# A graph layer's columns and maxima spread over partitions through DRAM instead of TensorE, with one buffer of reciprocals and nine of exponentials

## The chip, the core and the metric

The kernel runs on one core of a Trainium2 chip. A core has a matrix engine (TensorE, PE in the profile), a vector engine (VectorE, DVE), a scalar engine (ScalarE, ACT), GpSimd (POOL) and SyncE (SP), which here only issues DMAs. Each engine works through its own queue of instructions; semaphores between the queues keep the data in order. SBUF is the on-chip memory of 128 partitions, PSUM the memory that matmuls write into, DRAM the large memory outside. A DMA moves data between DRAM and SBUF or inside SBUF. The metric is the time of the kernel on the device in microseconds (us); lower is better.

## What is computed

The input x holds 32 independent items of 512 nodes with 512 features; adj is a 512 x 512 adjacency that all items share. Two layers follow each other, each with a residual and a layer norm:

```python
def layer0(X, A, W, a):                       # W: 512 x 256, a: 2 x 256 x 1
    h = einsum('bnf,fo->bno', X, W)
    e = einsum('bno,od->bnd', h, a[0]) + swapaxes(einsum('bno,od->bnd', h, a[1]), 1, 2)
    e = leaky_relu(e, 0.2) - 1e9 * (1 - A)
    alpha = softmax(e, axis=-1)
    return concatenate([einsum('bij,bjo->bio', alpha, h), h], axis=-1)

def layer1(h, adj, Wq, bq, Wk, bk, Wv, bv, Wo, bo):      # 8 heads of 64
    q, k, v = heads(h @ Wq.T + bq), heads(h @ Wk.T + bk), heads(h @ Wv.T + bv)
    s = where(adj == 0, -inf, einsum('bhqd,bhkd->bhqk', q, k) / 8)
    return merge(einsum('bhqk,bhkd->bhqd', softmax(s), v)) @ Wo.T + bo

x = layernorm(x + layer0(x, adj, W, a))
x = layernorm(x + layer1(x, adj, Wq, bq, Wk, bk, Wv, bv, Wo, bo))
```

In layer 0 the score of a pair of nodes is only a sum of two numbers, one for each node: a column "self" and a column "neigh" of 512 numbers. The change is about how such a column, which lies with one number in each partition, becomes a row that every partition holds.

## The kernel before

All arithmetic is in float32. An item b is handled whole: 512 nodes are four tiles of 128 partitions (NB = 4). The main loop runs over b, and inside it over four pairs of heads (hp = 0 to 3, "pairs" below). Into the four pairs of item b are woven layer 0 of item b + 1, the projection and column work of item b + 2, and the output projection (finish) of item b - 1, so that TensorE always has work.

The queues of TensorE, SyncE and VectorE keep the order in which the program text issues their instructions. The orders of ScalarE and GpSimd are set by the framework's scheduler, from its own estimate of when operands are ready. Tiles come from pools: `bufs` is the number of buffers behind a tag, and an instruction that writes a reused buffer waits until the earlier readers are done.

What each pair does on TensorE, in this order: scores of the tiles 0 and 1 (`ps`, head_scores), a first insert, scores of the tiles 2 and 3, then head_values of the pair before (`pav`), then a second insert. The inserts that matter here:

- pair 0: first insert l0_scores(b + 1) and project_v; second insert l0_rows(b + 1), project_v, and on other engines l0_add_h(b + 1) and l0_weights(b + 1).
- pair 1: l0_values(b + 1) (`po`), then project_two(b, 1) for the second half of the heads.
- pair 2: finish(b - 1) (`pf`).
- pair 3: store(b - 1), four l0_project(b + 2) (`ph`), then project_two(b + 1, 0) for the first heads of the next item.

For the scores VectorE takes, for each tile and head, a masked maximum out of PSUM into a tile p (tag "p"), ScalarE takes the exponential in place with its sum, and after all eight of a pair VectorE transposes them in blocks (head_blocks). Then VectorE takes the reciprocals of the sums (tot), SyncE writes them to DRAM (d_tot), and two GpSimd DMAs read them back into all partitions (inv), while SyncE issues 16 DMAs that move the transposed blocks (pt<-t). head_values of that pair, a pair later, multiplies by inv (VectorE, ot).

Layer 0 of an item:

- l0_project: `ph` = x W with two more columns for self and neigh; ScalarE copies it to h (L339 in the profile).
- l0_scores: row_of transposes a column, broadcast to 128 columns, against the identity: four matmuls of 128 x 128 leave the row of 512 numbers in every partition of a PSUM tile. `pn` is the neigh row; four masked maxima on VectorE write into throwaway tiles junk (tag "p"), and from them comes `most`, the maximum of each node. `pself` is the self row; ScalarE's Prelu adds neigh and takes the leaky ReLU into et (L366), and GpSimd adds the mask (L370).
- l0_rows: row_of turns `most` into the row `pl`.
- l0_weights: VectorE subtracts `pl` from et (L383), ScalarE takes the exponential (L384).
- l0_values: `po` = et times h, normalised and added to x by VectorE.

The tile et shares its one buffer with xt of the item after it, which l0_project reads in pair 3.

project_two computes two head pairs of q and k with seven partial products instead of eight. Its ScalarE copies p1, p5, p7 and u2 (L481) use the tag "p"; GpSimd adds p5 to p7 (L509); VectorE writes qk in four results of two operations each (L493), in the order result(0, 0), result(1, 1), result(0, 1), result(1, 0):

```python
        p7 = copy(b4, "p7")
        nc.gpsimd.tensor_tensor(p7, p7, p5, ALU.add)
        ...
        result(0, 0, b2, p1)
        product(b1, s_(1), t_(1), start=False)
        u2 = copy(b1, "u2")
        yield
        result(1, 1, b1, p7)
        product(b3, s_(2), b_(1, 1), start=False)
        yield
        result(0, 1, b3, u2)
```

The scores of the next item's pair 0 read qk of out[0], which result(0, 0) and result(0, 1) write.

Of the kernel before, what the change touches and what calls it, by code (L numbers as in the profile page):

```python
# [9 lines left out]
F32 = mybir.dt.float32  # L10
BF16 = mybir.dt.bfloat16
AF = mybir.ActivationFunctionType
ALU = mybir.AluOpType

P = 128
# [11 lines left out]
def kernel(  # L27
# [50 lines left out]
    D = F // H  # L78
    NB = N // P
    FC = F // P  # L80
    OC = F1 // P
    NP = H // 2
    SCALE = 1.0 / math.sqrt(D)
# [37 lines left out]
    st = {}  # L121
# [119 lines left out]
    def psum(name):  # L241
        return ps_m.tile([P, N], F32, name=name, tag="m")
# [98 lines left out]
    def l0_add_h(b):  # L341

        h_sb, z = st["h", b], st["x1", b]
        for i in range(NB):
            nc.gpsimd.tensor_tensor(
                z[:, i, F1:], z[:, i, F1:], h_sb[:, i, 2 : F1 + 2], ALU.add
            )

    def l0_scores(b):


        h_sb = st["h", b]
        pn = psum(f"pn_{b}")
        row_of(lambda i: h_sb[:, i, 1:2], pn)
        least = small.tile([P, NB], F32, name=f"least0_{b}", tag="least0", bufs=2)
        for i in range(NB):
            junk = prob.tile([P, N], F32, name=f"junk_{b}_{i}", tag="p", bufs=10)
            minus_max(junk, pn, mask0[:, i, :], least[:, i : i + 1])
        most = small.tile([P, NB], F32, name=f"most0_{b}", tag="most0", bufs=2)
        nc.vector.tensor_tensor(most, h_sb[:, :, 0], least, ALU.subtract)  # L360
        nc.vector.scalar_tensor_tensor(most, most, ALPHA, most, ALU.mult, ALU.max)
        pself = psum(f"pself_{b}")
        row_of(lambda i: h_sb[:, i, 0:1], pself)
        et = prob.tile([P, NB, N], F32, name=f"et_{b}", tag="et", bufs=1)
        for j in range(NB):
            nc.scalar.activation(  # L366
                et[:, j, :], pself, AF.Prelu, bias=h_sb[:, j, 1:2], alpha=ALPHA
            )
            engine = nc.vector if b == 0 and j >= 2 else nc.gpsimd
            engine.tensor_tensor(et[:, j, :], et[:, j, :], mask0t[:, j, :], ALU.add)  # L370
        st["l0", b] = et, most

    def l0_rows(b):
        _, most = st["l0", b]
        pl = psum(f"pl_{b}")
        row_of(lambda i: most[:, i : i + 1], pl)
        st["pl", b] = pl

    def l0_weights(b):
        et, _ = st["l0", b]  # L380
        pl = st.pop(("pl", b))
        for j in range(NB):
            nc.vector.tensor_tensor(et[:, j, :], et[:, j, :], pl, ALU.subtract)  # L383
            nc.scalar.activation(et[:, j, :], et[:, j, :], AF.Exp)  # L384

    def l0_values(b, i):
# [61 lines left out]
    def project_two(b, s):  # L448


        x1t, tx = st["x1t", b], st["tx", b]
        half = N // 2

        def product(ps, weights, moving, start=True):
            for k in range(2):
                for c in range(FC // 2):
                    nc.tensor.matmul(  # L457
                        ps[:, k * half : (k + 1) * half],
                        weights(k, c),
                        moving(c),  # L460
                        start=start and k == 0 and c == 0,
                        stop=c == FC // 2 - 1,
                        skip_group_check=True,
                    )

        def a_(i, f):
            cols = slice((2 * s + i) * P, (2 * s + i + 1) * P)
            return lambda k, c: (wq_sb, wk_sb)[k][:, 2 * f + c, cols]

        def s_(i):  # L470
            return lambda k, c: (wqx_sb, wkx_sb)[k][:, i, c, s, :]

        def b_(f, j):
            return lambda c: x1t[:, 2 * j : 2 * j + 2, 2 * f + c, :]

        def t_(i):
            return lambda c: tx[:, i, :, c, :]

        def copy(ps, name):
            t = prob.tile([P, N], F32, name=f"{name}_{b}_{s}", tag="p", bufs=10)  # L480
            nc.scalar.copy(t, ps)  # L481
            return t

        out = []
        for i in range(2):
            t = act.tile([P, 2, N], F32, name=f"qk_{b}_{2 * s + i}", tag="qk", bufs=2)
            st["qk", b, 2 * s + i] = t
            out.append(t)

        def result(i, j, ps, other):  # L490
            for k, bias in enumerate((bqs_sb, bk_sb)):
                cols = slice(k * half, (k + 1) * half)
                nc.vector.scalar_tensor_tensor(  # L493
                    out[i][:, k, j * half : (j + 1) * half],
                    ps[:, cols],
                    bias[:, 2 * s + i : 2 * s + i + 1],
                    other[:, cols],
                    ALU.add,
                    ALU.add,
                )  # L500

        b1, b3, b4 = (psum(f"pw{i}_{b}_{s}") for i in (1, 3, 4))
        product(b1, a_(0, 0), b_(0, 0))
        p1 = copy(b1, "p1")
        product(b3, s_(0), t_(0))
        p5 = copy(b3, "p5")
        product(b4, a_(1, 0), t_(2))
        p7 = copy(b4, "p7")
        nc.gpsimd.tensor_tensor(p7, p7, p5, ALU.add)  # L509
        b2 = psum(f"pw2_{b}_{s}")  # L510
        product(b2, a_(0, 1), b_(1, 0))
# [9 lines that stand above are left out]
        product(b4, a_(1, 1), t_(3), start=False)  # L521
        yield
        result(1, 0, b4, u2)
# [9 lines left out]
    def head_scores(b, hp, i):  # L533
        qk = st["qk", b, hp]
        if i == 0:
            st["t", b, hp] = prob.tile(
                [P, 4, 2, FC, NB, G], F32, name=f"t_{b}_{hp}", tag="t", bufs=1
            )
            st["tot", b, hp] = small.tile(
                [P, 2, NB], F32, name=f"tot_{b}_{hp}", tag="total", bufs=3  # L540
            )
        t, total = st["t", b, hp], st["tot", b, hp]
        pss = []
        for j in range(2):
            rows = slice(j * D, (j + 1) * D)
            ps = ps_s.tile([P, N], F32, name=f"ps_{b}_{hp}_{i}_{j}", tag="s")
            nc.tensor.matmul(  # L547
                ps, qk[rows, 0, i * P : (i + 1) * P], qk[rows, 1, :], start=True, stop=True
            )
            pss.append(ps)  # L550
        for j in range(2):
            name = f"{b}_{hp}_{i}_{j}"
            p = prob.tile([P, N], F32, name=f"p_{name}", tag="p", bufs=10)
            least = small.tile([P, 1], F32, name=f"least_{name}", tag="least", bufs=6)
            minus_max(p, pss[j], mask1[:, i, :], least)
            nc.scalar.activation(  # L556
                p, p, AF.Exp, bias=least, scale=-1.0, accum_out=total[:, j, i : i + 1]
            )
            st.setdefault(("p", b, hp), []).append((j, i, p))

    def head_blocks(b, hp):
        t, total = st.pop(("t", b, hp)), st.pop(("tot", b, hp))
        for j, i, p in st.pop(("p", b, hp)):
            transpose_blocks(t[:, :, j], i, p)
        nc.vector.reciprocal(total, total)
        d = dram.tile([2, P, NB], F32, name=f"d_tot_{b}_{hp}", tag="dtot")
        nc.sync.dma_start(d.rearrange("j p i -> p j i"), total)
        inv = act.tile([P, P, NB], F32, name=f"inv_{b}_{hp}", tag="inv", bufs=2)
        for j in range(2):
            nc.gpsimd.dma_start(inv[j * D : (j + 1) * D], d[j].partition_broadcast(D))  # L570
        st["inv", b, hp] = inv
        pt = prob.tile([P, 4, 2, FC, NB, G], F32, name=f"pt_{b}_{hp}", tag="pt", bufs=1)
        move_pair(pt, t)
        st["pt", b, hp] = pt
# [66 lines left out]
    masks0()  # L641
    l0_scores(0)
    l0_add_h(0)
    l0_rows(0)
    l0_weights(0)
    nc.vector.tensor_scalar(bqs_sb, bq_sb, SCALE, None, ALU.mult)
    sums = weight_sums()
# [13 lines left out]
    x1_first()  # L661
    l0_project(1, 2)
    l0_project(1, 3)
    x1_sums(0, nc.vector)
    project_v(0, 0)
    project_v(0, 1)
# [2 lines left out]
    for b in range(B):  # L669
        more = b < B - 1  # L670
        for hp in range(NP):
# [22 lines left out]
            elif hp == 2:  # L694
                if b > 0 and more:
                    finish(b - 1, 0)
                if b > 0 and more:
                    add_bias(b + 1)
            else:
                if b > 0:  # L700
                    if not more:
                        finish(b - 1, 3)
                    store(b - 1)
                if b + 2 < B:
                    for i in range(NB):
                        l0_project(b + 2, i)
                if b == 0:
                    project_v(1, 0)
            head_scores(b, hp, 2)
# [4 lines left out]
            if before is not None:  # L714
                head_values(*before)
            if hp == 0:
                if more:
                    l0_rows(b + 1)
                else:
                    project_v(b, 1)  # L720
                project_v(b, 2)
                project_v(b, 3)
# [99 lines left out]
```

## Time and profile before

| | us |
|---|---|
| median of 3 runs | 3209.63 |
| lowest and highest | 3207.91 and 3209.9 |
| the profiled execution | 3209.49 |
| span of its trace | 3207.7 |

Some groups of instructions of the trace that the change touches:

| engine, instruction | count | busy us | mean ns |
|---|---|---|---|
| TensorE L326, matmuls for pn | 128 | 20.8 | 285 |
| TensorE L326, matmuls for pself | 128 | 19.2 | 273 |
| TensorE L326, matmuls for pl | 128 | 21.7 | 294 |
| VectorE L287, junk from pn | 128 | 80.6 | 686 |
| VectorE L383, et minus pl | 128 | 79.2 | 680 |
| ScalarE L366, Prelu into et | 128 | 76.4 | 672 |
| GpSimd L370, mask added to et | 126 | 141.6 | 1156 |
| GpSimd L509, p5 added to p7 | 64 | 83.7 | 1308 |
| GpSimd L570, issue of inv | 256 | 134.4 | 528 |

The matmuls of a group overlap each other in the record, so the mean of one times the count is not the time that the group takes; that is read from the starts in a timeline. A timeline line gives the start, the length, the engine, the line of the program, the tiles and a count, and in brackets how long the engine had been idle before and what ended that. SPq is SyncE's queue of DMA issues; a DMA's landing comes later than its issue.

### The profile page before, as it was taken

Reading aid. Unit: us, or ns where it says so; the run is one execution under the profiler, and the core shown is the slowest. Engines: PE = TensorE matmul, PEld = TensorE weight load, DVE = VectorE, ACT = ScalarE, POOL = GpSimd, SP = SyncE. Lnnn points to the kernel's source line nnn. Section 1 sums busy time; section 2 is a strip of 40 time slices with the busy share of each in tenths; the row PEclk is TensorE's granted clock in tenths of the full one; section 3 lists DMA queues with packets and bytes.
Section 4 is the critical chain, followed back from the end, with each engine's and each line's share of the span. In section 5 each row is a group of like instructions: output and inputs, shape, how many; then the busy total and the mean of one; then the engine's idle time right before and its main releaser. Section 6 shows DMA issues by size and latency. Waiting matters only on the chain.

```text
span 3207.7 us, 41188 instructions
## 1 busy us (share of the span) xinstructions
PE 3163.1 (99%) x12216; PEld 1806.1 (56%) x12216; DVE 2451.1 (76%) x5665; ACT 1332.1 (42%) x3026; POOL 759.1 (24%) x869
## 2 busy tenths in 40 slices
PE   7999999999999999999999999999999999999997
PEld 5555555556556555555565565555555655655543
DVE  5788777877777877778777778877787777788775
ACT  3444443434444444434344444444343444444432
POOL 1322222221222222222222222222222122222210
PEclk9999999999999999999999999999999999999999
DMA  5565555555556555555555555555555555555554
GB/s 148 129 157 127 139 141 150 129 144 143 142 129 152 148 127 137 143 150 128 140 146 141 129 150 149 127 139 141 150 129 145 142 141 129 152 146 128 125 137 115
DMA packets 226094, 446.12 MB, mean 139 GB/s; under 512 B 81680, under 2 KB 84240, under 8 KB 225872
## 3 DMA queue, kind: packets, MB, share of 16 engines
q1 hardware_dynamic: 213408, 409.65, 50.5%
q0 software_dynamic: 12464, 33.84, 4.0%
q8 instruction: 99, 1.62, 0.2%
q14 instruction: 123, 1.01, 0.1%
HBM read 108.27 MB, written 34.08 MB: 44 GB/s over the span
## 4 chain that ended last, share of the span: by engine, by line
PE 95%; DVE 1%; SPq 1%; DMA 0%; issue 0%; ACT 0%; DVEq 0%; ACTq 0%
PE pw L457 25%; PE ps L547 15%; PE pav L582 14%; PE pv L239 14%; PE pf L603 13%; PE ph L239 7%; PE po L391 7%; SPq L319 1%; PE pl L326 1%; PE pn L326 1%; DVE t L302 0%; PE pself L326 0%; DMA pt<-t 0%; DVE p L287 0%; DVE x1t_b L302 0%
## 5 line engine op out<-in xcount | busy, mean ns | idle before, releaser
L556 ACT ACTIVATE p<-p,least 128x512 f32<-128x512 f32 x1024 | 725.9, 710 | 485.1 <-DVE least L287 416.4
L287 DVE CUSTOM_DVE_ANT_0 p<-ps,mask 128x512 f32<-128x512 f32 x1024 | 643.0, 684 | 314.0 <-PE ps L547 314.0
L302 DVE STREAM_TRANSPOSE t<-p 128x512 f32<-128x512 f32 x1024 | 621.8, 674 | 0.0
L547 PE MATMUL ps<-qk 64*128 64x512 f32 x2048 | 511.6, 615 | 2.4 <-DVE least L287 2.4
L582 PE MATMUL pav<-pt,v 128*64 128x512 f32 x2048 | 467.7, 598 | 5.3 <-DMA pt<-t 2.7
L603 PE MATMUL pf<-wo_sb,ot 128*128 128x512 f32 x1024 | 459.6, 602 | 5.6 <-DVE ot L590 5.6
L239 PE MATMUL pv<-wv_sb,x1t 128*128 128x512 f32 x1024 | 451.3, 593 | 0.0
L570 POOL DMA_DIRECT2D inv<-d_tot x256 | 134.4, 528 | 1296.2 <-DMA d_tot<-tot 712.2
L603 PEld LDWEIGHTS pf<-wo_sb,ot 128*128 128x128 f32 x1024 | 190.0, 191 | 272.4 <-issue 264.4
L547 PEld LDWEIGHTS ps<-qk 64*128 64x128 f32 x2048 | 177.8, 186 | 265.3 <-issue 207.5
L582 PEld LDWEIGHTS pav<-pt,v 128*64 128x64 f32 x2048 | 136.5, 136 | 321.1 <-issue 250.2
L239 PEld LDWEIGHTS pv<-wv_sb,x1t 128*128 128x128 f32 x1024 | 190.1, 191 | 216.0 <-issue 215.9
L239 PE MATMUL ph<-w_sb,xt 128*128 128x258 f32 x1024 | 236.9, 389 | 5.0 <-ACT x1t L422 4.7
L391 PE MATMUL po<-h,et 128*128 128x257 f32 x1024 | 232.6, 385 | 1.6 <-issue 1.6
L239 PEld LDWEIGHTS ph<-w_sb,xt 128*128 128x128 f32 x1024 | 194.8, 193 | 57.0 <-DVE mv L253 22.0
L258 ACT ACTIVATE rstd<-mv,eps 128x4 f32<-128x4 f32 (+1 forms) x70 | 20.8, 297 | 489.3 <-DVE mv L253 487.2
L391 PEld LDWEIGHTS po<-h,et 128*128 128x128 f32 x1024 | 193.4, 191 | 51.8 <-issue 25.4
L370 POOL TENSOR_TENSOR et<-et,mask0t 128x512 f32<-128x512 f32 x126 | 141.6, 1156 | 304.0 <-ACT et L366 304.0
L446 POOL TENSOR_TENSOR x<-x,bo_sb 128x512 f32<-128x512 f32 x128 | 158.4, 1269 | 190.4 <-DVE x1t_b L302 170.6
L493 DVE SCALAR_TENSOR_TENSOR qk<-pw,bqs_sb,p 128x256 f32<-128x256 f32 x128 | 61.6, 481 | 184.2 <-PE pw L457 116.7
L556 ACT ACTIVATION_READ_ACCUMULATOR p<-p,least 128x1 f32 x1024 | 191.2, 187 | 0.0
L252 DVE BATCH_NORM_STATS2 stats<-x 128x6 f32<-128x512 f32 x256 | 177.5, 693 | 13.9
(99 smaller groups left out, 3762.2 us busy)
## 6 DMA issues: line engine op xcount, KB each, us to landing
pt<-t SPq DMA_DIRECT2D x2048, 128.0 KB, 3.4
x<-in_x_dram SPq DMA_DIRECT2D x32, 1024.0 KB, 5.8
inv<-d_tot POOLq DMA_DIRECT2D x256, 128.0 KB, 3.8
xt<-in_xt_dram SPq DMA_DIRECT2D x31, 1024.0 KB, 5.4
x1t<-x1t_b SPq DMA_DIRECT2D x496, 64.0 KB, 2.0
out_dram<-x SPq DMA_DIRECT2D x31, 1024.0 KB, 4.3
d_tot<-tot SPq DMA_DIRECT2D x128, 4.0 KB, 2.1
xt<-in_xt_dram SPq DMA_DIRECT2D x4, 256.0 KB, 7.4
```

The lines of the kernel that those rows point to most:

```text
L239: nc.tensor.matmul(ps, lhs(c), rhs(c), start=(c == 0), stop=(c == FC - 1))
L252: nc.vector.bn_stats(stats, z[:, i, :])
L287: nc.vector.tensor_tensor_reduce(out=out, in0=scores, in1=mask, scale=-1.0, scalar=MIN_INIT, op0=ALU.add, op1=ALU.min, accum_out=least,)
L302: nc.vector.transpose(t[:, :, :, i, :].rearrange("p r c q -> p c r q"), src.rearrange("p (c r k) -> p c r k", r=4, k=G),)
L370: engine.tensor_tensor(et[:, j, :], et[:, j, :], mask0t[:, j, :], ALU.add)
L391: nc.tensor.matmul(po, et[:, j, i * P : (i + 1) * P], h_sb[:, j, 2:], start=(j == 0), stop=(j == NB - 1),)
L446: nc.gpsimd.tensor_tensor(z[:, i, :], z[:, i, :], bo_sb, ALU.add)
L457: nc.tensor.matmul(ps[:, k * half : (k + 1) * half], weights(k, c), moving(c), start=start and k == 0 and c == 0, stop=c == FC // 2 - 1, s ...
L547: nc.tensor.matmul(ps, qk[rows, 0, i * P : (i + 1) * P], qk[rows, 1, :], start=True, stop=True)
L556: nc.scalar.activation(p, p, AF.Exp, bias=least, scale=-1.0, accum_out=total[:, j, i : i + 1])
L582: nc.tensor.matmul(po[j * D : (j + 1) * D, :], st["v", b, c][:, head * D : (head + 1) * D], pt[:, :, j, c, :, :].rearrange("p g i q -> p g ...
L603: nc.tensor.matmul(ps, st["ot", b, c][:, i * P : (i + 1) * P], wo_sb[:, c, :], start=(c == 0), stop=(c == FC - 1),)
```

## The change

For all items but the first, the two columns and the maxima go to DRAM and come back as rows that every partition holds. SyncE writes the columns with one DMA each, one number at a time (l0_columns, behind l0_project in pair 3), and one GpSimd DMA reads both back into rows (128 x 2 x 512). The maxima go the same way from l0_scores into row. The reads of pn, pself and pl become reads of these SBUF tiles; l0_rows is gone. Item 0 keeps row_of. The exponentials have nine buffers instead of ten, inv one instead of two.

```diff
+    PB = 9
...
+    def l0_columns(b):
+
+        h_sb = st["h", b]
+        d = dram.tile([2, N], F32, name=f"d_att_{b}", tag="datt")
+        with nc.allow_non_contiguous_dma(reason="1024 numbers"):
+            for k in range(2):
+                nc.sync.dma_start(d[k].rearrange("(i p) -> p i", p=P), h_sb[:, :, k])
+        rows = prob.tile([P, 2, N], F32, name=f"rows_{b}", tag="rows", bufs=1)
+        nc.gpsimd.dma_start(rows, d.partition_broadcast(P))
+        st["rows", b] = rows
+
     def l0_scores(b):
         h_sb = st["h", b]
-        pn = psum(f"pn_{b}")
-        row_of(lambda i: h_sb[:, i, 1:2], pn)
+        if b == 0:
+            pself, pn = psum("pself"), psum("pn")
+            row_of(lambda i: h_sb[:, i, 1:2], pn)
+            row_of(lambda i: h_sb[:, i, 0:1], pself)
+        else:
+            rows = st.pop(("rows", b))
+            pself, pn = rows[:, 0], rows[:, 1]
         least = small.tile([P, NB], F32, name=f"least0_{b}", tag="least0", bufs=2)
         for i in range(NB):
-            junk = prob.tile([P, N], F32, name=f"junk_{b}_{i}", tag="p", bufs=10)
+            junk = prob.tile([P, N], F32, name=f"junk_{b}_{i}", tag="p", bufs=PB)
             minus_max(junk, pn, mask0[:, i, :], least[:, i : i + 1])
...
-        pself = psum(f"pself_{b}")
-        row_of(lambda i: h_sb[:, i, 0:1], pself)
         et = prob.tile([P, NB, N], F32, name=f"et_{b}", tag="et", bufs=1)
...
-        st["l0", b] = et, most
-
-    def l0_rows(b):
-        _, most = st["l0", b]
-        pl = psum(f"pl_{b}")
-        row_of(lambda i: most[:, i : i + 1], pl)
-        st["pl", b] = pl
+        if b == 0:
+            row = psum("pl")
+            row_of(lambda i: most[:, i : i + 1], row)
+        else:
+            d = dram.tile([N], F32, name=f"d_most_{b}", tag="dmost")
+            with nc.allow_non_contiguous_dma(reason="512 numbers"):
+                nc.sync.dma_start(d.rearrange("(i p) -> p i", p=P), most)
+            row = prob.tile([P, N], F32, name=f"row_{b}", tag="row", bufs=1)
+            nc.gpsimd.dma_start(row, d.partition_broadcast(P))
+        st["l0", b] = et, row
 
     def l0_weights(b):
-        et, _ = st["l0", b]
-        pl = st.pop(("pl", b))
+        et, row = st["l0", b]
         for j in range(NB):
-            nc.vector.tensor_tensor(et[:, j, :], et[:, j, :], pl, ALU.subtract)
+            nc.vector.tensor_tensor(et[:, j, :], et[:, j, :], row, ALU.subtract)
             nc.scalar.activation(et[:, j, :], et[:, j, :], AF.Exp)
...
-        inv = act.tile([P, P, NB], F32, name=f"inv_{b}_{hp}", tag="inv", bufs=2)
+        inv = act.tile([P, P, NB], F32, name=f"inv_{b}_{hp}", tag="inv")
...
     l0_project(1, 2)
     l0_project(1, 3)
+    l0_columns(1)
...
                     for i in range(NB):
                         l0_project(b + 2, i)
+                    l0_columns(b + 2)
...
             if hp == 0:
-                if more:
-                    l0_rows(b + 1)
-                else:
+                if not more:
                     project_v(b, 1)
```

The tiles of head_scores and project_two take `bufs=PB` in the same way.

More of the change, by code (lines that the diff above doesn't have):

```diff
@@ L479, in copy @@
         def copy(ps, name):
-            t = prob.tile([P, N], F32, name=f"{name}_{b}_{s}", tag="p", bufs=10)
+            t = prob.tile([P, N], F32, name=f"{name}_{b}_{s}", tag="p", bufs=PB)
             nc.scalar.copy(t, ps)
@@ L552, in head_scores @@
             name = f"{b}_{hp}_{i}_{j}"
-            p = prob.tile([P, N], F32, name=f"p_{name}", tag="p", bufs=10)
+            p = prob.tile([P, N], F32, name=f"p_{name}", tag="p", bufs=PB)
             least = small.tile([P, 1], F32, name=f"least_{name}", tag="least", bufs=6)
@@ L643 @@
     l0_add_h(0)
-    l0_rows(0)
     l0_weights(0)
```

## The prediction

> **What bounds the kernel now.** I read the page first (busy shares, chain of waits), then the timeline of each engine over one steady batch, then the granted clock around the few places where TensorE rests.
>
> ```profile
> span 3207.7 us, 41188 instructions
> PE 3163.1 (99%) x12216; PEld 1806.1 (56%) x12216; DVE 2451.1 (76%) x5665; ACT 1332.1 (42%) x3026; POOL 759.1 (24%) x869
> PE 95%; DVE 1%; SPq 1%; DMA 0%; issue 0%; ACT 0%; DVEq 0%; ACTq 0%
> ```
>
> TensorE is busy for 99% of the span and carries 95% of the chain that ended last. So TensorE work that goes is worth its own length, unless a wait takes its place. The TensorE timeline from the end of pair 3 of one batch into pair 0 of the next (start, length, instructions):
>
> ```profile
> 1023.96 1.99 PE L547 MATMUL ps<-qk 64*128 64x512 f32 x8
> ...
> 1040.79 1.03 PE L457 MATMUL pw<-tx,wk_sb 128*128 128x256 f32 x4
> 1041.75 1.99 PE L547 MATMUL ps<-qk 64*128 64x512 f32 x8
> 1043.66 0.65 PE L326 MATMUL pn<-ident,h 128*128 128x128 f32 x4
> 1044.15 0.60 PE L326 MATMUL pself<-ident,h 128*128 128x128 f32 x4
> 1044.59 7.03 PE L239 MATMUL pv<-wv_sb,x1t 128*128 128x512 f32 x16
> ...
> 1057.05 0.65 PE L326 MATMUL pl<-ident,most 128*128 128x128 f32 x4
> 1057.54 7.03 PE L239 MATMUL pv<-wv_sb,x1t 128*128 128x512 f32 x16
> ```
>
> There is no gap: each group starts as the one before it ends, and the period from pn to pn is 98.03 us (1043.66 to 1141.69) in all middle batches. The same stretch on VectorE, GpSimd and SyncE:
>
> ```profile
> 1039.13 0.48 DVE L493 SCALAR_TENSOR_TENSOR qk<-pw,bqs_sb,p 128x256 f32<-128x256 f32 x1 [1.51 <-ACT u L481]
> 1039.53 0.48 DVE L493 SCALAR_TENSOR_TENSOR qk<-pw,bk_sb,p 128x256 f32<-128x256 f32 x1
> 1040.13 0.48 DVE L493 SCALAR_TENSOR_TENSOR qk<-pw,bqs_sb,u 128x256 f32<-128x256 f32 x1
> 1040.53 0.47 DVE L493 SCALAR_TENSOR_TENSOR qk<-pw,bk_sb,u 128x256 f32<-128x256 f32 x1
> ```
> ```profile
> 1034.66 1.04 POOL L570 DMA_DIRECT2D inv<-d_tot  x2 [20.11 <-DMA d_tot<-tot]
> 1035.72 1.28 POOL L509 TENSOR_TENSOR p<-p,p 128x512 f32<-128x512 f32 x1
> 1047.27 4.50 POOL L370 TENSOR_TENSOR et<-et,mask0t 128x512 f32<-128x512 f32 x4 [10.27 <-ACT et L366]
> ```
> ```profile
> 1032.58 0.36 SPq L567 DMA_DIRECT2D d_tot<-tot  x1
> ```
>
> Two things are to be seen. First, the scores of the next batch (ps at 1041.75) need qk, whose last needed part is written at 1040.53 and done at 1041.00: 0.75 us to spare. Second, GpSimd adds p7 to p5 (L509) directly behind the inv DMAs, at 1035.72, and the mask additions to et come after, because et's ScalarE step waits for pself on TensorE.
>
> **What the Trainium skill says.** PSUM — Partial Sum Buffer, Engine vs sequencer instructions: the queues of ScalarE, VectorE and GpSimd are "strict FIFO". The trace agrees: GpSimd sits 20.11 us before inv, waiting for d_tot. SBUF — State Buffer, Who interferes with whom: a VectorE operation with two SBUF inputs contends with a GpSimd operation that reads SBUF. The trace agrees: the tiny "most" (L361) has a minimum of 161 ns and a median of 1079 ns, in the steady batch while L370 runs on GpSimd. DMA: Bandwidth & Descriptors, Anatomy of one DMA: about 2 us fixed plus bytes. The page has 2.1 us for 4 KB of d_tot, 5.4 to 5.8 us for 1 MB. TensorE: Matmul & The Clock Gate, Part 1: an idle window of about 3.4 us throttles the clock to half. The trace agrees: after 3.48 us without work (23.0 to 26.48) the granted clock falls to half until 32.5 us.
>
> ```profile
> 22.00:23.00 1.00, 1.00 (x10) 1.00 1.05 387
> ...
> 26.00:27.00 1.00, 0.52 (x3) 0.55 1.13 369
> 27.00:28.00 1.00, 0.57 (x3) 0.50 1.04 172
> ```
> (stretch, its length, TensorE busy, granted clock, DMA share, GB/s)
>
> **The change part by part.**
>
> *Removed from TensorE.* pn and pself take 0.93 us (1043.66 to 1044.59), pl 0.49 us (1057.05 to 1057.54): 1.42 us in each of 31 batches, 44.0 us in all. All of it is on the bound.
>
> *What moves by itself.* ScalarE and GpSimd are not in a handwritten order, and in the order of the changed kernel as built they change. ScalarE's Prelu on et now needs rows instead of pself, so it moves from pair 0 into the end of pair 3, between the copies p1, p5, p7 of project_two. GpSimd's four mask additions move with it, ahead of p7's addition: from the boundary to batch 2 on, up to that to batch 30 (29 boundaries), GpSimd has rows, inv, inv, et x4, p7. At the boundary to batch 1 et stands before inv, where GpSimd waits for d_tot anyhow; I cost it at nothing.
>
> *The new wait.* p7 is read by the second result on VectorE, result(1,1). Behind it in VectorE's queue stands result(0,1), which the next scores need. In the steady batch: inv starts at 1034.66 and ends 1035.70; four mask additions take 4.49 (the row above, ending 1040.2); p7's addition 1.28 (1041.5); four result operations at a pitch of 0.40 with 0.47 for the last, and 0.17 for the two handovers (estimate), 1.84 (1043.35). TensorE was to start at 1041.75, so it waits 1.6 us. Written as a rule: inv start + 8.70 us. Inv starts when d_tot lands, 2.08 to 3.6 us after its issue, and the distance from inv to ps over these boundaries in the trace is 5.57 to 7.09 us, mean 6.5. So the wait is 1.6 to 3.1 us, mean 2.2, and 29 boundaries cost 64 us. TensorE has nothing else in its queue to do meanwhile and no slack later to give it back: d_tot's issue hangs on TensorE's own ps of 1023.96 (8.6 us before it in every batch).
>
> *Added transfers at the end of pair 3.* d_att: two SyncE DMAs of 512 single numbers each, issued after the last h copy (1024.44). Nothing stands behind them until d_tot at 1032.58; the store ahead of them (issue 1021.11, 4.3 us) ends about then. By d_tot's 2.1 to 3.6 us and a second issue 0.6 to 0.8 us later they land 3.0 to 4.7 us after the copy. Then rows: an inv DMA lands in 3.8 us for 128 KB; the step from 64 KB (2.0 us) to 1 MB (5.6 us) is 3.75 us per 1000 KB, so 512 KB lands in about 5.2 us. Rows are there 8.2 to 9.9 us after the copy, at 1032.6 to 1034.3. Prelu 1 (0.65) then ends by 1035.0 and the first mask addition at 1035.7 does not wait. The copy p1 follows Prelu 1 (0.58) and ends by 1035.6; TensorE reuses its bank at 1036.47. So nothing, with about 0.7 us left at the bad end. But rows may slow d_tot, whose packets come as it ends: 0 (its data is in) to 1 us (their tails overlap in full); I take 0.2 us, 6 us in all.
>
> *Added transfers in pair 0.* most is done at 1049.56, or 1.2 us earlier now that L370 has left. d_most lands within 3.6 us, by 1053.2; GpSimd reaches it behind three additions of h to x, which wait for x (issued 1043.43, 5.8 us) and end about 1051. The row of 256 KB lands by about 1057.8 against its reader at 1060.95. Nothing; if it were 4 us later, po at 1066.42 would begin to wait for the last exponential (1064.34).
>
> *VectorE reads rows and row in SBUF instead of PSUM.* Eight operations per batch may now contend with GpSimd. L370 has moved off; the additions of h to x (0.65 each) may hit one or two, up to 1.3 us. VectorE rests 3.15 us before 1052.71 and 2.23 us before 1065.66, which shrink by the 0.93 and 0.49 that TensorE is faster. Nothing.
>
> *One inv buffer.* The inv DMA must wait for the previous ot. ot ends at 1033.44, d_tot lands at 1034.66: 1.2 us hidden in every pair, since ot stands right behind the reciprocal whose result d_tot carries.
>
> *Nine buffers of p.* Eight are held up to the transposes (first ends by 1028.3), p1 takes the ninth, p5 the first that is free; p5 is copied at 1033. In pair 0 four p and four junk fit. Nothing.
>
> **Sum.** 3207.7 - 44.0 + 64 + 6 = 3233.7; with 1.8 outside the span (the profiled execution took 3209.49) 3235.5. That execution stands 0.14 below the median of 3209.63, so I say 3235.
>
> **The rivals.**
>
> *A, the forecast:* p7 behind the mask additions, a wait of 1.5 to 3.5 us: 3207 to 3265. 62%.
>
> *B, the wait grows and drags the clock.* For: the longest computed waits (3.1 us, plus contention) come near the 3.48 us that halved the clock; 6 us at half speed lose 3 us. Should half of the boundaries fall, 14 x 3 = 42: 3277. Rows later than 1035 add their delay one for one; 1 us is 29 us: 3264. Against: the gaps of 1.42 and 1.14 us near the end leave the clock at 1.00, and most waits are near 1.6 to 2.5 us. 17%.
>
> *C, the removed work counts in full (the other side).* If p7's addition ends less than 2.85 us later than before (2.1 us until VectorE wants it, 0.75 to spare), TensorE does not wait: 3209.5 - 44 = 3165.5. This takes mask additions that are over before d_tot lands, rows landing by about 1030, and a GpSimd order with et first. For: the boundary to batch 1 has it. Against: the built order of the other 29. 16%.
>
> *D, in between:* only the longest waits show, about 1 us each, 29 us: 3194. 5%.
>
> **How the numbers follow.** The time is A's, 3235. The range 3205 to 3280 holds A and most of B; left out are C, D and B's end. 0.2% is 6.4 us, about what a measurement can tell from no change. Faster: C and nearly all of D, 0.20. Within: A's low end, 0.08. Slower: 0.72.
>
> **What would show it.** In the changed profile: TensorE's timeline without pn, pself and pl in the middle batches, but with a wait of some 2 us before the first ps of each batch, released by qk on VectorE; VectorE's result(1,1) released by GpSimd's p; on GpSimd inv, et x4, p in one block; the granted clock still near 1.00. A period of about 99.0 us (98.03 - 1.42 + 2.4) against 98.03. Wrong would be no wait before ps (C), a wait for rows on ScalarE, a wait before po, or a clock below 0.97 (B).

## The result and the profile after

| | us |
|---|---|
| before, median of 6 runs | 3209.41 |
| after, median of 6 runs (3425.68 to 3440.49) | 3431.85 |
| ratio, 95% interval | 1.0698 (1.0681 to 1.0715) |
| forecast | 3235, range 3205 to 3280 |

The change makes the kernel 7% slower. The direction was forecast, the size was not: the loss is 222 us where 25 were expected. Below, a batch is one pass of the loop over b, and a boundary is the end of pair 3 with the start of the next pair 0. The page of the kernel after (span, busy time of each engine, shares of the chain that ended last):

```profile
span 3423.9 us, 40601 instructions
...
PE 3200.4 (93%) x11844; PEld 1808.1 (53%) x11844; DVE 2417.2 (71%) x5665; ACT 1339.2 (39%) x3026; POOL 807.3 (24%) x931
...
PE 73%; issue 12%; DMA 7%; DVE 3%; ACT 2%; POOL 1%; SPq 1%; ACTq 0%; DVEq 0%; POOLq 0%
```

Two numbers stand out. TensorE has 372 matmuls fewer than before (11844 against 12216) and is yet busy for longer, 3200.4 us against 3163.1. And it is idle for 3423.9 - 3200.4 = 223.5 us, where it was idle for 44.6. Four lines of the waits of the same kernel (engine, tile and line, what it waits for; total us, times, longest):

```profile
POOL rows L358 <- DMA d_att<-h: 587.1, 31, 22.0
POOL row L394 <- DMA d_most<-most: 370.1, 31, 19.8
ACT et L381 <- issue: 354.0, 30, 15.4
PE pw L474 <- ACT p L498: 157.3, 29, 8.9
```

The new wait of TensorE is not ahead of ps, the scores of the next batch, where the forecast put it. It is ahead of pw, a product in the middle of project_two, and it comes once in each of 29 batches with a mean of 5.4 us. Its releaser is the copy p1 on ScalarE. The timeline of one boundary of the kernel after shows why, in four pieces for TensorE, SyncE's queue, GpSimd and ScalarE:

```profile
1112.52 1.03 PE L474 MATMUL pw<-x1t,wk_sb 128*128 128x256 f32 x4
1120.56 2.04 PE L474 MATMUL pw<-tx,wqx_sb 128*128 128x256 f32 x4 [7.01 <-ACT p L498]
...
1127.80 1.99 PE L564 MATMUL ps<-qk 64*128 64x512 f32 x8
```
```profile
1101.38 0.92 SPq L356 DMA_DIRECT2D d_att<-h  x2
```
```profile
1112.59 0.55 POOL L358 DMA_DIRECT2D rows<-d_att  x1 [21.25 <-DMA d_att<-h]
...
1120.04 4.49 POOL L385 TENSOR_TENSOR et<-et,mask0t 128x512 f32<-128x512 f32 x4 [5.67 <-ACT et L381]
1124.49 1.26 POOL L526 TENSOR_TENSOR p<-p,p 128x512 f32<-128x512 f32 x1
```
```profile
1100.98 0.37 ACT L340 COPY h<-ph 128x258 f32<-128x258 f32 x1 [1.37 <-PE ph L240]
...
1119.22 0.72 ACT L381 ACTIVATE et<-rows,h 128x512 f32<-128x512 f32 x1 [13.46 <-issue]
1119.85 0.57 ACT L498 COPY p<-pw 128x512 f32<-128x512 f32 x1
```

Read it from the bottom up. TensorE resumes at 1120.56 because p1 has just left its PSUM bank, which the next product needs (L498 at 1119.85). In the kernel before, ScalarE made the last copy to h and the copy p1 at these times:

```profile
1024.07 0.37 ACT L339 COPY h<-ph 128x258 f32<-128x258 f32 x1 [1.37 <-PE ph L239]
...
1031.55 0.58 ACT L481 COPY p<-pw 128x512 f32<-128x512 f32 x1 [2.70 <-PE pw L457]
```

There p1 is copied 7.1 us after the last copy to h has ended (1031.55 against 1024.44); in the kernel after it is 18.5 us (1119.85 against 1101.35). It stood in ScalarE's queue behind the first Prelu (L381), which waited for rows; the profile shows this as 13.46 us of idle time that ends with "issue", that is, without naming what ScalarE waited for. Rows came late: the two d_att DMAs were issued at 1101.38, right behind the last copy to h, and GpSimd could issue the read of rows only when they had landed, at 1112.59. That is 11.2 us after the copy, and Prelu starts 17.9 us after it. The forecast had 3.0 to 4.7 us and 8.2 to 9.9 us for these two. The landing of the two DMAs is seen directly in the list of issues (KB each, median us from issue to landing):

```profile
rows<-d_att POOLq DMA_DIRECT2D x31, 512.0 KB, 5.8
row<-d_most POOLq DMA_DIRECT2D x31, 256.0 KB, 4.7
d_tot<-tot SPq DMA_DIRECT2D x128, 4.0 KB, 2.5
d_att<-h SPq DMA_DIRECT2D x62, 2.0 KB, 8.4
d_most<-most SPq DMA_DIRECT2D x31, 2.0 KB, 8.3
```

A DMA of 2 KB takes more than three times as long as one of 4 KB in the same queue.

The gap has a second price. The stretches of the same boundary in the kernel after (stretch, its length, TensorE busy with its matmuls, the other engines, granted clock as a share of TensorE's full clock, DMA share, GB/s):

```profile
1113.40:1120.50 7.10, 0.15 (x1) 0.00 (x0) 0.05 (x1) 1.28 (x3) 1.43 (x3) 0.79 0.99 230
1120.50:1124.20 3.70, 3.64 (x9) 2.95 (x10) 0.83 (x2) 2.72 (x5) 3.70 (x4) 0.50 0.96 223
1124.20:1127.80 3.60, 3.60 (x17) 2.91 (x16) 1.66 (x4) 0.59 (x1) 1.55 (x2) 0.97 0.94 303
```

After the gap of 7.01 us the clock is 0.50 for 3.7 us, and 9 matmuls take the time of 17. Behind each of the 29 gaps the mean clock of the next 3.6 us lies between 0.50 and 0.66. This is why TensorE has less work and more busy time.

### The profile page after: what moved, and what is told of

Same layout as the page of the kernel before. It is cut to its first block, busy times and chain, and to the rows that moved or that the text cites. A ratio compares the mean times of both kernels' runs of the same rounds, so it can differ in the third digit from the quotient of the medians.

```text
span 3423.9 us, 40601 instructions
## 1 busy us (share of the span) xinstructions
PE 3200.4 (93%) x11844; PEld 1808.1 (53%) x11844; DVE 2417.2 (71%) x5665; ACT 1339.2 (39%) x3026; POOL 807.3 (24%) x931
## 4 chain that ended last, share of the span: by engine, by line
PE 73%; issue 12%; DMA 7%; DVE 3%; ACT 2%; POOL 1%; SPq 1%; ACTq 0%; DVEq 0%; POOLq 0%
PE pw L474 17%; PE pf L620 12%; PE ps L564 11%; PE pv L240 10%; PE pav L599 9%; PE po L408 7%; PE ph L240 6%; DMA d_att<-h 3%; DMA d_most<-most 2%; DMA row<-d_most 1%; POOL et L385 1%; SPq L320 1%; DVE junk L288 1%; ACT p L573 1%; DVE p L288 1%
## 5 line engine op out<-in xcount | busy, mean ns | idle before, releaser
L474 PE MATMUL pw<-tx,wqx_sb 128*128 128x256 f32 x512 | 159.6, 441 | 162.3 <-ACT p L498 157.3
L408 PE MATMUL po<-h,et 128*128 128x257 f32 x1024 | 239.6, 391 | 16.7 <-ACT et L401 15.0
L381 ACT ACTIVATE et<-rows,h 128x512 f32<-128x512 f32 x124 | 85.9, 719 | 366.0 <-issue 354.0
L474 PEld LDWEIGHTS pw<-tx,wqx_sb 128*128 128x128 f32 x512 | 108.5, 219 | 188.7 <-issue 168.1
```

Source lines behind the costliest of these rows:

```text
L381: nc.scalar.activation(et[:, j, :], pself, AF.Prelu, bias=h_sb[:, j, 1:2], alpha=ALPHA)
L408: nc.tensor.matmul(po, et[:, j, i * P : (i + 1) * P], h_sb[:, j, 2:], start=(j == 0), stop=(j == NB - 1),)
L474: nc.tensor.matmul(ps[:, k * half : (k + 1) * half], weights(k, c), moving(c), start=start and k == 0 and c == 0, stop=c == FC // 2 - 1, s ...
```

## The experiments

Four questions: which of the two transfers, that of the columns or that of the maxima, costs the time, whether it costs it through the place to which the scheduler moved Prelu, why so small a DMA lands so late, and whether the rest of the change is free.

### The scheduler's move taken back (hold)

One tiny VectorE copy of the neigh column, placed in pair 0, is made the bias of Prelu. Prelu and the mask additions then become ready in pair 0, where they stood before, behind p1, p5 and p7.

```diff
+        neigh = h_sb[:, :, 1]
+        if b > 0:
+            neigh = small.tile([P, NB], F32, name=f"neigh_{b}", tag="neigh", bufs=2)
+            nc.vector.tensor_copy(neigh, h_sb[:, :, 1])
...
-                et[:, j, :], pself, AF.Prelu, bias=h_sb[:, j, 1:2], alpha=ALPHA
+                et[:, j, :], pself, AF.Prelu, bias=neigh[:, j : j + 1], alpha=ALPHA
```

> The changed kernel, with one tiny VectorE copy of the neigh column in pair 0 that Prelu reads as its bias, so that ScalarE's Prelu and GpSimd's mask additions go back to pair 0, behind p1, p5, p7. Theory 1 (the single-number DMAs land late, Prelu waits for rows, and the copy p1 stands behind Prelu in ScalarE's queue): the waits of pw on p1 and the half clock behind them vanish; 3209.5 - 44 + 15 to 30 for po on the late row = 3180 to 3196. Theory 2 (the extra transfers and two SBUF inputs slow the kernel wherever Prelu stands): stays above 3400.

Measured: 3250.9 us, ratio 1.0129 (1.0112 to 1.0146). The wait of TensorE for p1 is gone, and with it 181 us of the loss of 222. So the price hung on where Prelu and the mask additions stand. hold moves both, on ScalarE and on GpSimd; that it was ScalarE's queue is read from the releaser of pw in the kernel after, the copy p1. But the time is some 60 us above what was expected, and the waits of this kernel name what took the place:

```profile
DVE et L404 <- DMA row<-d_most: 160.4, 31, 7.8
PE po L412 <- ACT et L405: 55.7, 28, 11.1
```

Now po waits for the exponentials of et (28 times, 15.5 of the 55.7 us in the first two batches), these for the subtraction on VectorE, and that one for row. Around one batch of this kernel, on SyncE's queue and on GpSimd:

```profile
1076.33 0.36 SPq L396 DMA_DIRECT2D d_most<-most  x1
```
```profile
1073.51 5.00 POOL L389 TENSOR_TENSOR et<-et,mask0t 128x512 f32<-128x512 f32 x4 [7.68 <-ACT et L385]
1078.71 1.93 POOL L346 TENSOR_TENSOR x<-x,h 128x256 f32<-128x256 f32 x3 [0.20 <-DMA x<-in_x_dram]
1085.68 0.56 POOL L398 DMA_DIRECT2D row<-d_most  x1 [5.04 <-DMA d_most<-most]
```

d_most is issued at 1076.33, 8.38 us after the start of the batch's ps (1067.95), and the read of row is issued 9.35 us later. In the kernel after, d_most is issued 6.57 us after its ps (1134.37 against 1127.80): with the mask additions gone to pair 3, the maxima are done 1.8 us earlier. The difference is nearly all in the two small VectorE operations that make most: they take 0.99 and 1.08 us in hold, where the mask additions run beside them, and 0.17 and 0.16 us in the kernel after. The slow landing was already at the edge in pair 0 (po waits in 7 batches of the kernel after, in 28 of hold); that these 1.8 us are what pushes it over was not tried alone.

### Each half alone (cols_only, most_only)

cols_only is the kernel after with the maxima back on TensorE:

```diff
-                nc.sync.dma_start(d.rearrange("(i p) -> p i", p=P), most)
...
-            nc.gpsimd.dma_start(row, d.partition_broadcast(P))
...
+        row_of(lambda i: most[:, i : i + 1], row)
```

most_only is the kernel after with the two columns back on TensorE, so that only the maxima go by way of DRAM:

```diff
+        row_of(lambda i: h_sb[:, i, 1:2], pn)
...
+        row_of(lambda i: h_sb[:, i, 0:1], pself)
...
-                    l0_columns(b + 2)
```

> The changed kernel with the maxima back on TensorE (pl), the columns still through DRAM. Theory 1: the loss is all in the columns: gain 29 (0.93 x 31), waits of pw on p1 about 160, half clock about 80: 3410 to 3440. Rival (the row of maxima, late before its reader, carries half or more of the loss): under 3320.

> The changed kernel with pn and pself back on TensorE, the maxima through DRAM. Theory 1: gain 15 (0.49 x 31), lost again in part by po waiting for the exponentials (0 to 17): 3195 to 3212. Rival (the row of maxima carries half or more of the loss): above 3310.

Measured: cols_only 3483.51 us, ratio 1.0851 (1.083 to 1.0873); most_only 3226.57 us, ratio 1.0051 (1.0031 to 1.0071). Both are above their expected ranges. The columns alone carry the loss, and more than all of it: TensorE waits for p1 for 204.3 us in cols_only (29 times, up to 9.7 us) against 157.3 in the kernel after. The lists of issues say where the 47 us come from: in cols_only d_att lands in 9.0 us and rows in 6.7, in the kernel after in 8.4 and 5.8, which is 1.5 us in each of 29 batches, or 44. Why they land later there stays open.

The maxima alone cost half a per cent, nearly all of it at the start: most_only has gaps of 11.9 and 4.4 us before po in the first two batches, and its span is 16.9 us longer than that of the kernel before. In most of the later batches its period is 97.64 us, against 98.02, so that 0.38 of the 0.49 us of TensorE are gained; some take longer, above all late ones, up to 98.9.

### What makes a small DMA late (probe, pitch)

Both kernels are the kernel before with one DMA more in each batch, at the place of d_att in pair 3, whose result nothing reads. In probe four forms take turns: as in the change (d_far); the four numbers of a partition side by side (d_near); the same in runs of 16 bytes from the contiguous tile most (d_runs); each number 512 bytes from the next (d_apart).

```diff
+                d = dram.tile([N], F32, name=f"d_far_{b}", tag="d0")
+                nc.sync.dma_start(d.rearrange("(i p) -> p i", p=P), h_sb[:, :, 0])
...
+                d = dram.tile([P, NB, P], F32, name=f"d_apart_{b}", tag="d3")
+                nc.sync.dma_start(d[:, :, 0], h_sb[:, :, 0])
```

> The kernel before, with one more DMA per batch in pair 3, where l0_columns stands, that nobody reads: by turns d_far (512 single numbers, those of a partition 512 bytes apart in DRAM, as d_att), d_near (the same numbers, those of a partition side by side), d_apart (512 single numbers, each 512 bytes from the next), d_runs (128 runs of 16 bytes out of a packed tile). If single numbers are slow by themselves: far, near and apart land in 6 to 10 us, runs in 2 to 4. If it is the place in the queue behind the store: all four in 6 to 10. If it is neighbours that share a line of DRAM: apart lands in 2 to 4 and near is as slow as far or slower. Time 3205 to 3215 in all cases, since nobody waits.

Measured: 3211.61 us in one run, so the probe does not disturb. The list of issues of probe (KB each, median us to landing; 7 or 8 of each form):

```profile
d_runs<-most SPq DMA_DIRECT2D x8, 2.0 KB, 4.4
d_apart<-h SPq DMA_DIRECT2D x8, 2.0 KB, 2.2
d_far<-h SPq DMA_DIRECT2D x7, 2.0 KB, 9.0
d_near<-h SPq DMA_DIRECT2D x7, 2.0 KB, 7.3
```

d_far and d_apart move the same 512 single numbers from the same tile at the same place in the same queue. So it is neither the number of elements, nor their size, nor the store ahead of them: it is how the numbers lie in DRAM. Two things do not fit the theory of neighbours as it was put: d_near lands faster than d_far (7.3 against 9.0 us) where it should have been as slow or slower, and the runs of 16 bytes of d_runs take 4.4 us where d_tot, which writes more of such runs, takes 2.1 us in the same kernel. Both stay open. In pitch only the distance is changed, in the order of the change:

```diff
+        pitch = (1, 4, 16, 32, 64, 128)[b % 6]
...
+            d = dram.tile([NB, P, pitch], F32, name=f"d_{4 * pitch}B_{b}", tag=f"d{pitch}")
+            nc.sync.dma_start(d[:, :, 0].rearrange("i p -> p i"), h_sb[:, :, 0])
```

> The kernel before with one more DMA in each batch whose result nothing reads: 512 single numbers of h, laid down as the change lays them, in the order of the partitions, but 4, 16, 64, 128, 256 or 512 bytes from one to the next, by turns, at the place of d_att in pair 3. The time should stay near 3210 us. Theory one, numbers that fall into the same small stretch of DRAM wait for each other: the landing is 8.5 to 9 us at 4 bytes, falls in one step at the size of that stretch[...], and is 2.1 to 2.5 us at every pitch above it. Theory two, the time goes by how many numbers share a larger block, whatever its size: the landing falls step by step from 9 to 2 us over the six pitches, and 256 bytes is still above 3 us. Theory three, only the order of the layout counts (a partition's four numbers far apart against side by side): all six land in 8.5 to 9 us.

Measured: 3210.85 us in one run. The list of issues of pitch, where the name tells the distance from one number to the next (5 of each):

```profile
d_64B<-h SPq DMA_DIRECT2D x5, 2.0 KB, 2.2
d_128B<-h SPq DMA_DIRECT2D x5, 2.0 KB, 1.9
d_256B<-h SPq DMA_DIRECT2D x5, 2.0 KB, 1.9
d_512B<-h SPq DMA_DIRECT2D x5, 2.0 KB, 1.8
d_4B<-h SPq DMA_DIRECT2D x5, 2.0 KB, 10.1
d_16B<-h SPq DMA_DIRECT2D x5, 2.0 KB, 2.9
```

The third theory falls, since the order of the layout is the same in all six, and so does the second, which had more than 3 us left at 256 bytes. Nor is it quite the first: most of the fall comes between 4 and 16 bytes (the slowest landing at 16 bytes was 3.3 us, the fastest at 4 was 8.8), and 64 bytes are only a little better than 16. What is shown is that 512 single 4-byte writes of this kernel land some 8 us later when they are packed than when they lie 64 bytes or more apart. That writes into one small stretch of DRAM wait for each other is the natural reading; the runs show the effect of the distance, not the mechanism.

### The change with the slow landing taken out (after_apart, hold_apart)

after_apart is the kernel after, with each number written 512 bytes from the next, into a DRAM tile that is filled with zeros once. The reads take a contiguous piece of that tile of the same size as before, so rows and row hold zeros and a few of the numbers: both kernels leave out the columns and maxima of layer 0 and serve for their times alone. Behind the filling, the instructions of every engine and their order stay those of the kernel after. hold_apart is the same with the edit of hold.

```diff
+    d_att = dram.tile([2 * N, P], F32, name="d_att", tag="datt", bufs=1)
...
-                nc.sync.dma_start(d[k].rearrange("(i p) -> p i", p=P), h_sb[:, :, k])
+                nc.sync.dma_start(
+                    d_att[k * N : (k + 1) * N, 0].rearrange("(i p) -> p i", p=P), h_sb[:, :, k]
+                )
...
+            d_att[N - 4 : N + 4].rearrange("r q -> (r q)").partition_broadcast(P),
```

> The changed kernel with the same instructions in the same order, but the single numbers of d_att and d_most go 512 bytes apart in DRAM, and rows and row read 4 KB and 2 KB in one piece from there, so they hold zeros and a few of the numbers: the maxima and columns of layer 0 are not computed. If neighbours sharing a line of DRAM are what makes the landing late, d_att and d_most land in 2 to 4 us, rows are there by 9.5 us behind the h copy, the waits of pw on p1 go, and what is left is the forecast's chain, p7 behind the mask additions: a wait of 1.6 to 3.1 us before ps in 29 batches, 3220 to 3245. If p7's chain costs nothing either: 3166 to 3185. If the order of Prelu and p1 alone is the loss: above 3300.

> As after_apart, with Prelu held in pair 0 by the small VectorE copy; the same part of layer 0 is not computed. Theory (only late landing and the moved Prelu cost anything; one inv buffer, nine p, SBUF reads and 760 KB more of traffic per batch are free): 3165 to 3178. Rival (these together cost): 3185 or more.

Measured: after_apart 3239.17 us, ratio 1.0088 (1.0073 to 1.0103); hold_apart 3175.88 us, ratio 0.9891 (0.9876 to 0.9906). The list of issues of after_apart:

```profile
rows<-d_att POOLq DMA_DIRECT2D x31, 512.0 KB, 3.9
...
d_att<-h SPq DMA_DIRECT2D x62, 2.0 KB, 2.1
d_most<-most SPq DMA_DIRECT2D x31, 2.0 KB, 1.8
```

The fast landing of the writes takes 193 us off the kernel after and puts it near the forecast of 3235; the read of rows is faster with it (3.9 us against 5.8), and the two were not parted. The timeline of one boundary of after_apart, on TensorE, VectorE and GpSimd:

```profile
1052.39 1.99 PE L576 MATMUL ps<-qk 64*128 64x512 f32 x8 [1.40 <-DVE qk L522]
```
```profile
1050.67 0.48 DVE L522 SCALAR_TENSOR_TENSOR qk<-pw,bqs_sb,p 128x256 f32<-128x256 f32 x1 [3.88 <-POOL p L538]
```
```profile
1043.83 1.07 POOL L599 DMA_DIRECT2D inv<-d_tot  x2 [6.55 <-DMA d_tot<-tot]
1044.92 4.49 POOL L396 TENSOR_TENSOR et<-et,mask0t 128x512 f32<-128x512 f32 x4
1049.38 1.26 POOL L538 TENSOR_TENSOR p<-p,p 128x512 f32<-128x512 f32 x1
```

Here is the wait that the prediction drew, step for step: inv, four mask additions, p7, result(1, 1), and ps late. From the start of inv to ps it is 1052.39 - 1043.83 = 8.56 us; the rule of the forecast said 8.70.

hold_apart takes this wait away too, and its middle batches, all of 96.81 us, have no wait left on TensorE. Its page:

```profile
span 3175.1 us, 40700 instructions
PE 3128.0 (99%) x11844; PEld 1772.3 (56%) x11844; DVE 2467.6 (78%) x5696; ACT 1347.0 (42%) x3026; POOL 812.3 (26%) x935
```

So one buffer of inv, nine of p, the reads out of SBUF and the added traffic of 768 KB in a batch cost no time that shows in a middle batch. The period is 96.81 us against 98.02: 1.21 us gained of the 1.42 that the transposes took. The rest is seen in the timeline: the two pv groups that followed on pself and pl lasted 7.03 us each, and last 7.13 now that they follow on ps and pav.

The same page sets the account of the kernel after. Both have the same 11844 matmuls. The kernel after is busy for 3200.4 - 3128.0 = 72.4 us more, at the lower clock, and idle for 223.5 - 47.1 = 176.4 us more, of which 157.3 are the wait for p1. The sum is the difference of the spans, 248.8.

The four kernels side by side (medians in us):

| | packed writes | writes 512 bytes apart |
|---|---|---|
| Prelu in pair 3 | 3431.85 (after) | 3239.17 (after_apart) |
| Prelu held in pair 0 | 3250.9 (hold) | 3175.88 (hold_apart) |

Counted from hold_apart, the moved Prelu alone costs 63 us and the slow landing alone 75, but both together 256. The late transfer is dear because of the place of its reader, and the place because of the late transfer.

### Versions that keep the gain (hold_cols, hold_small)

In hold the columns have some 20 us of cover before their first reader in pair 0 (in hold_cols d_att is issued at 1021.85 and the first junk starts at 1042.81); the maxima have 11 (in the kernel before most is done at 1049.56 and pl is first read at 1060.95). hold_cols is hold with the maxima back on TensorE (the edit of cols_only). hold_small is hold with one small transpose of most (128 x 4 to 4 x 128) and a copy, so that d_most is written in four runs of 512 bytes; its edit, against hold:

```diff
+            nc.tensor.transpose(row[:NB, :P], most, ident)
...
+            nc.vector.tensor_copy(four, row[:NB, :P])
...
-                nc.sync.dma_start(d.rearrange("(i p) -> p i", p=P), most)
+            nc.sync.dma_start(d.rearrange("(i p) -> i p", p=P), four)
```

> Columns through DRAM as in the changed kernel, Prelu held in pair 0, the maxima back on TensorE (pl). Theory: rows have 20 us and are never late, 0.93 us x 31 = 29 gained: 3178 to 3186. Rival (the added traffic delays pt or inv so that TensorE waits elsewhere): 3195 or more.

> Columns through DRAM, Prelu held in pair 0; the maxima go through one small transpose on TensorE (128 x 4 into 4 rows of 128) behind the third scores of pair 0, a VectorE copy and a DMA of four runs of 512 bytes, then row as in the change. Theory: 0.93 + 0.49 - 0.15 = 1.27 us x 31 = 39 gained if the row lands in time; d_most lands in about 2 to 3 us: 3168 to 3182. Rival (GpSimd issues row behind the mask additions and po still waits 1 us or more): 3195 to 3240.

Measured: hold_cols 3189.77 us, ratio 0.9934 (0.9919 to 0.9949), with a period of 97.20 us; hold_small 3197.03 us, ratio 0.9952 (0.9935 to 0.9969), with a period of 97.22 us and a slower second batch (102.23 us from one po to the next, with a gap of 5.2 us before a pav). Both are faster than the kernel before, by 0.7% and 0.5%, and both are above what was expected. In hold_cols d_att still lands in 9.3 us and rows in 6.4, and nothing on TensorE waits for them; it gains 0.82 us in a batch and not 0.93, since one pv group lasts 7.13 us. hold_small lies in the range of its rival, but not for the rival's reason: po does not wait in its middle batches. Its one small transpose between two groups of ps costs TensorE 0.40 us (2.32 us from this ps to pav, where hold_apart has 1.92), not 0.15, and so nearly as much as the four transposes of pl with 0.49.

## Why the prediction was wrong in size, and its direction right by another path

**The step that failed** is the landing of d_att: "By d_tot's 2.1 to 3.6 us and a second issue 0.6 to 0.8 us later they land 3.0 to 4.7 us after the copy." d_tot was taken as the nearest row of the profile, and it was the wrong row: it writes four numbers at a time (tot of one partition and head), and d_att writes one. Measured are 11.2 us at the boundary shown. To that, rows added 6.6 us (1112.59 to 1119.22) where 5.2 were taken. Together Prelu came 17.9 us after the copy, 8.0 later than the bad end of 9.9; less the 0.7 us that the forecast had left, 7.3 us, and the wait of this boundary is 7.01. So the chain "Rows are there ... Prelu 1 ... the copy p1 ... its bank" was the right chain; the term at its head was too small by 6.5 us and more, and no upper bound was kept for it, though the view did not show the operation. The sum of a fixed 2 us and the bytes that stands beside it (the Trainium skill, DMA: Bandwidth & Descriptors, Anatomy of one DMA) could not warn of this: the page gives it for DMAs that GpSimd issues, d_att is one of SyncE's, and pitch has 1.8 to 10.1 us for the same 2 KB.

**The forecast wait (A)** is real and was hidden. In the kernel after, result(1, 1) waits 4.46 us for p7 at the boundary shown, but TensorE is itself so late that ps loses nothing. So the direction was right, but in the kernel after not for the reason given. With the slow landing out, ps waits for qk in 29 batches, 54.4 us in all, where 64 were forecast. That after_apart then falls near 3235 is in part luck: against the kernel before it the sum was to add 26 us (44 off, 70 on) and 26.9 are measured, but as 36.4 off and 63.3 on. Of the 70, the 6 us for a slower d_tot are not seen (d_tot lands in 2.0 us, before in 2.1), and the 8 us by which TensorE is busier than in hold_apart were not in it.

**The rival B** had the right mechanism: "Rows later than 1035 add their delay one for one; 1 us is 29 us". The delay was 5.4 us in the mean, 157 us, not 1. All four signs of being wrong that the prediction named came with it: hardly a wait of ps for qk (0.9 us in all), a wait on ScalarE for rows, a wait before po (7 batches), and a clock below 0.97 (0.968 in the trace). Its clock term was right too: these gaps halve the clock, and it cost 72 us. The passage cited from the Trainium skill (TensorE: Matmul & The Clock Gate, Part 1) agrees with the gap of 7.01 us and the 0.50 behind it. The 3.48 us that the prediction took from the trace as the gap that halves the clock are no sharp bound, though: in the kernel before a gap of 2.89 us (before pl, at 81.37) has 0.50 behind it, and in hold one of 2.26 us (before po, at 1980.78) has 0.50 and one of 3.20 us (before po, at 398.07) has 1.00.

**The maxima.** "d_most lands within 3.6 us" failed by the same term: the read was issued 9.3 us after it (1143.68 against 1134.37), 5.7 us more. The threshold beside it, "if it were 4 us later", fits: po waits in 7 batches of the kernel after for 15.0 us, and in 28 of hold.

**What was costed at nothing** was right for inv, p and the reads out of SBUF (hold_apart). **The removed work** was put at 44.0 us; hold_apart gains 36.4 (3212.26 - 3175.88), mostly since 1.21 us are gained in a batch and not 1.42. Two slips in the working changed nothing: rival A's 3207 to 3265 leaves out the 1.8 us outside the span and the 6 us of d_tot, and the clock at the start of the kernel before is back at 32.9 us, not 32.5.

## What to carry to other kernels

A price from the nearest row of a profile did not hold here, since d_tot and d_att differ in how their addresses lie; for an operation that the profile does not show, keep an upper end and carry it through to the engine that would wait. When an operand is moved from PSUM to a transfer, look for where the scheduler puts its reader: an in-order queue charges the lateness of the transfer to everything behind that reader, and a small dependence that holds the reader back, as in hold, was worth 181 us. In this kernel a column spread by way of DRAM paid where it had its full latency as cover (hold_cols, 20 us for the columns). With 11 us (the maxima) it was at the edge: most_only gained in most batches and lost more in the first two, and in hold po waited in 28.

## What was not expected of the hardware

512 single numbers of 4 bytes, written in the order of the change, land in 8.7 to 11.5 us when they are packed (probe and pitch), in 2.9 us in the median at 16 bytes from one to the next, and in 1.8 to 2.2 us in the median from 64 bytes on. The reading DMAs are slower in the kernel after too (rows 5.8 us against 3.9 in after_apart); there they run beside inv and pt with the DMA engines at 0.99 of their time, which may be the reason and was not tried alone. A group of 16 matmuls took 7.13 or 7.03 us depending on the group ahead of it, and one transpose of 128 x 4 between two groups of ps took 0.40 us where four of 128 x 128 in a row took 0.49.
